# A graph layer on one core: search ahead of everything, no branch and no copies of the edges, a gather that waits for a maximum, and other moves

## The chip, the cores and the metric

The kernel runs on one core of a Trainium2 chip. The metric is the device time of one execution in microseconds (us). The core's engines run in parallel, each on its own queue of instructions: TensorE (PE, with the loading of weights shown apart as PEld), VectorE (DVE), ScalarE (ACT), GpSimd (POOL) and SyncE (SP). Transfers are issued by SP, ACT and POOL. Each queue is served in order, and an instruction that waits for a semaphore holds all that stand behind it on its engine.

## The reference, cut to what matters

```
theta_x = (x_dst - x_src) @ theta_w.T + theta_b      # x_dst = x[dst], x_src = x[src]
phi_x   = x_src @ phi_w.T + phi_b
e       = relu(theta_x + phi_x)                      # one row of 256 for each edge
out     = segment_max(e, dst, num_segments=6250)     # 0 where a node has no edge
return layernorm(x + out)
```

There are 6250 nodes with 256 features in fp32, and 100000 edges. The edges come sorted by `dst`. The row of an edge is A[dst] + B[src], with A = x·thetaᵀ plus both biases and B = x·(phi − theta)ᵀ. Since A is the same for all edges of a node, the maximum over a node's edges is A plus the maximum of the B rows of its sources.

## The kernel before, in words

**B.** At the start x is read in shares of four columns of 128 nodes (`x_q`, loads by SP), transposed on PE, copied by ACT, multiplied (L764) and stored as `b_rows` in DRAM by 13 stores that ACT issues (L784).

**Two parts.** Part 1 are the first 1130 nodes: eight columns of 128 and a rest, called `LAST`, so nine columns. Part 2 are the last 5120 nodes: 40 columns.

**Part 1** cuts its edges into 128 chunks of 146 steps, one chunk for each partition. POOL fetches one step of all chunks with one indirect DMA (L513): two groups of eight steps from x, which are then turned into B in place, and 130 steps from `b_rows`. DVE keeps a running maximum along the steps (L691), and the rows go to `maxima_1`. A node's result is the row of its last step; its place is worked out in `node_place` and `places_1`.

**Part 2** first builds a table of edges by node on DVE (`fill_table`, L930 on). For this it needs the window of 800 edges that belongs to each partition's nodes: `search_edges` (L615 to L647) finds where it begins with two small matmuls and counts, and `gather_run` fetches `dst_w` and `src_w` from there. The source nodes are cut into 17 slots of 383 rows. For two slots at a time, `choice` (L990 on) picks at most one edge per node and slot; `wanted` transposes the chosen rows on PE (L1034) and stores them as `chosen_rows`. A slot has five parts of 1024 nodes, 85 in all. `slot_part` loads the chosen rows spread over the partitions (`want`, L1061), makes one-hots from them (`hot`, by ACT in an Abs and a Relu at L1067 and L1068, or by DVE at L1065), and PE multiplies them with the slot's B rows (`terms`), 24 matmuls of 512 columns a part (L1075). DVE takes the maximum into `acc` (L1086).

**The list.** Edges that no slot took go to a list. `list_pieces` packs their words on DVE and writes them to DRAM (L1212); three `list_run` gathers read them back in even chunks. Then come 232 gathers of B rows (`list_src`), with their maxima (L691) written to `maxima_2`. The loop over the 30 list groups of eight gathers also issues the slot parts that are left, evenly over the groups.

**The end.** `rows_of` (L1270 on) loads x for up to eight columns (`x_f`, five tiles in `x_ring`), gathers a row from `maxima_1` or `maxima_2` for each column, and a `piece` of two columns makes A on PE (x transposed at L1292, two products a column at L1299, the bias at L1302), transposes `acc` (L1309) for part 2 and adds up. `normalise` (L1318 on) makes the layer norm and stores the rows. `Shares` interleaves the pieces with the norms. `LAST` is done within the last four list groups; part 1's eight columns and part 2's 40 (in widths 8, 8, 8, 4, 4, 4, 2, 2) come after the list.

**What sets the order.** A scheduler places the instructions of each engine by the order in which the program issues them and by extra dependencies written by hand: `in_turn` keeps POOL's DMAs in the order of the program; `behind_in_order` puts an instruction behind another on the same engine without a semaphore. `next_group_1` issues a group of part 1's gathers, the maxima of the group before it, a `node_place` and some slot parts. The gathered rows live in `gathered`, a ring of six tiles of eight steps.

**The start.** Besides loading the edges' `dst` in two layouts, ACT's queue copies `dst` and `src` to `dst_list` and `src_list` in DRAM and writes pads behind them. DVE counts descents in `dst`; at L653 every engine reads that count, and a branch at L654 sorts the edges if it isn't zero. With the given edges it is zero, and the branch is not taken. A second branch, at the kernel's end, takes a general path if any assumption failed.

Of the kernel before, what the change touches and what calls it, by code (L numbers as in the profile page):

```python
# [55 lines left out]
STEPS = 8  # L56
RING = 6
# [17 lines left out]
EARLY_STEPS = 6  # L75
X_RING = 5
# [351 lines left out]
def gnn_kernel(ctx: ExitStack, tc: tile.TileContext, x, src, dst, theta_w, theta_b, phi_w, phi_b, out):  # L428
# [72 lines left out]
    paced = [0]  # L501
# [14 lines left out]
    def gather(to, table, offsets):  # L516
        one = indirect(to, table, bass.IndirectOffsetOnAxis(ap=offsets, axis=0))
        for _ in range(paced[0]):
            in_turn(iota(pause, 1, 0, 0))
        return one  # L520
# [14 lines left out]

    def gather_group(i, table, a=0, b=STEPS):
        t0, n = groups[i]
        if i not in ring_tiles:
            ring_tiles[i] = gathered.tile([P, STEPS, D], FP, name="g")
        return [  # L540
            gather(ring_tiles[i][:, k, :], table, src_1[:, t0 + k : t0 + k + 1]) for k in range(a, min(b, n))
        ]

    gather_group(of_x[0], x, 0, EARLY_STEPS)


    dst_1 = const.tile([P, T1 + 2], I32, name="dst_1")
    early = body.enter_context(ExitStack())
    search = early.enter_context(tc.tile_pool(name="search", bufs=1))
# [5 lines left out]
    whole = [[E // P, P], [1, E // P]]  # L555
    rest = [[E % P, 1], [1, E % P]]
    pads = const.tile([P, 2, 8], I32, name="pads")
    nc.vector.memset(pads[:, 0, :], 0)
    nc.vector.memset(pads[:, 1, :], ID_MASK)
# [7 lines left out]
    ident = const.tile([P, P], FP, name="ident")  # L567
    make_identity(nc, ident)
    ones = const.tile([P, 1], FP, name="ones")
    nc.vector.memset(ones, 1.0)  # L570
    flags = const.tile([1, 2], I32, name="flags")
# [14 lines left out]
    first_node = const.tile([P, 1], FP, name="first_node")  # L586
    iota(first_node, 0, N1, TILES)
    columns = const.tile([P, 3, P], FP, name="columns")
    iota(columns[:, 0, :], Q1, 0, 0)
    iota(columns[:, 1, :], 1, P * Q1, 0)  # L590
    iota(columns[:, 2, :], TILES, N1 - 1 + TILES, 0)
    lowest_rows = search.tile([P, 2 * D], FP, name="lowest_rows")
    nc.vector.memset(lowest_rows, LOWEST)
    nc.sync.dma_start(maxima_1[NONE_1 : NONE_1 + 1, :], lowest_rows[0:1, :D])
    nc.sync.dma_start(maxima_2[0:1, :], lowest_rows[0:1, :D])
    list_pads = search.tile([4, OWN_LIST], I32, name="list_pads")
    nc.vector.memset(list_pads, PAD_WORD)
    nc.sync.dma_start(flat(list_words, 0, [[OWN_LIST, 1], [1, OWN_LIST]]), list_pads[:1, :])
    nc.sync.dma_start(flat(list_words, (P + 1) * OWN_LIST, [[OWN_LIST, 3], [1, OWN_LIST]]), list_pads[:3, :])
    bad = const.tile([P, 9], FP, name="bad")  # L600

    descents = search.tile([P, T + 1], FP, name="descents")
    nc.vector.tensor_tensor(descents, dst_i[:, : T + 1], dst_i[:, 1:], op=ALU.is_gt)
    n_descents = search.tile([P, 1], FP, name="n_descents")
    nc.vector.tensor_reduce(n_descents, descents, AX.X, ALU.add)
    add_up(n_descents, flags[:, 0:1])

    ids = search.tile([P, T + 2], FP, name="ids")  # L610
# [10 lines left out]

    def search_edges():

        nc.vector.tensor_copy(ids[:, : T + 1], dst_i[:, 1:])
        iota(ids[:, T + 1 :], 0, 0, T)
# [3 lines left out]
        nc.vector.tensor_scalar(hot0, columns[:, 2, :], low0, None, op0=ALU.is_ge)  # L629
        nc.vector.scalar_tensor_tensor(hot0, columns[:, 2, :], ids[:, T : T + 1], hot0, op0=ALU.is_lt, op1=ALU.mult)  # L630
        cut = 2 * D
        for i, (a, b, n) in enumerate(((cut, T + 2, T), (0, cut, cut))):
            pp = misc()
            nc.tensor.matmul(pp[:, : b - a], hot0, ids[:, a:b], start=True, stop=True)
            nc.vector.tensor_scalar(
                descents[:, a:n], pp[:, : n - a], last_node, None, op0=ALU.is_le, op1=ALU.add, accum_out=counts[:, i : i + 1]
            )
# [3 lines left out]
        nc.vector.tensor_scalar(window, counts[:, 0:1], float(E - WINDOW), None, op0=ALU.min)  # L641
# [7 lines left out]
    with (  # L649
        tc.tile_pool(name="sort", bufs=1) as sort,  # L650
        tc.tile_pool(name="ps_sort", bufs=2, space=PSUM) as ps_sort,
    ):
        n_unsorted = nc.values_load(flags[0:1, 0:1])  # L653
        with tc.If(n_unsorted > 0):  # L654
            sort_edges(nc, sort, ps_sort, src, dst, src_list, dst_list, ident)
            load_chunks(nc.sync, dst_i, dst_list, T, EDGES)
            load_chunks(nc.sync, dst_1, dst_list, T1, EDGES)
            load_rows(nc.scalar, src_1, src_list, P * T1)
            latest[0] = None
            gather_group(of_x[0], x)  # L660
            search_edges()
    latest[0] = None
# [4 lines left out]


    ids_1 = const.tile([P, T1 + 3], FP, name="ids_1")
    nc.vector.tensor_copy(ids_1[:, : T1 + 2], dst_1)  # L670
# [11 lines left out]
    def run(part, g, n, caps, t0, to, gathers=(), carry_row=None):  # L682


        for k in range(n):
            t = t0 + k if part == 1 else LIST_CHUNK - 1 - t0 - k
            if last[part] is not None:
# [10 lines left out]
                if part == 2 and latest_part[0] is not None:  # L698
                    behind_in_order(one, latest_part[0], "VectorE's order")
            last[part] = g[:, k, :]  # L700
# [14 lines left out]
    with (  # L715
        tc.tile_pool(name="prep", bufs=1) as prep,
        tc.tile_pool(name="x_in", bufs=4) as x_in,
# [8 lines left out]
        for i, b in enumerate((theta_b, phi_b)):  # L726
            nc.sync.dma_start(biases[:, i, :], flat(b, 0, [[0, P], [1, D]]))
        bias = prep.tile([P, D], FP, name="bias")
        rest = prep.tile([P, D], FP, name="rest")
        high_part = prep.tile([P, D], FR, name="high_part")  # L730
        nc.vector.tensor_add(bias, biases[:, 0, :], biases[:, 1, :])
        nc.vector.tensor_copy(high_part, bias)
        nc.vector.tensor_tensor(rest, bias, high_part.bitcast(FP), op=ALU.subtract)
        nc.vector.tensor_scalar(bias, high_part.bitcast(FP), ident[:, 0:1], None, op0=ALU.mult)
        nc.vector.scalar_tensor_tensor(bias_terms, rest, ident[:, 1:2], bias, op0=ALU.mult, op1=ALU.add)
        pick_one = prep.tile([P, 1], FP, name="pick_one")
        nc.vector.tensor_add(pick_one, ident[:, 0:1], ident[:, 1:2])
        nc.vector.tensor_copy(pick, pick_one.to_broadcast([P, P]))
        nc.vector.tensor_sub(w_in[:, 0], w_in[:, 0], w_in[:, 1])
        for i in range(2):  # L740
            for c in range(KC):
# [3 lines left out]
                nc.vector.tensor_copy(weights[:, :, i, c * P : (c + 1) * P], ps[:, 0])  # L745
# [520 lines left out]
    def gather_carry():  # L1266
# [3 lines left out]
        return carry_row  # L1270


    def rows_of(part, j0, n, ps_tile):


        share = part, j0, n
# [221 lines left out]
```

## Time and profile before

| | us |
|---|---|
| median of three runs | 727.39 |
| lowest, highest | 723.31, 733.8 |
| profiled execution | 728.03 |
| its span | 726.2 |
| busy: PE | 623.0 (86%) |
| busy: DVE | 623.9 (86%) |
| busy: ACT | 485.5 (67%) |
| busy: POOL | 486.0 (67%) |

The span is the time from the first to the last instruction that the profile shows. The profiled execution has its own time, 1.8 us over its span, and it is this execution whose rows are added up below. A row of a group reads: line, engine, operation, output and inputs with their shapes, how often, then busy time, mean nanoseconds of one, and the idle time of the engine ahead of them with what ended most of it. A row of a timeline reads: start, duration, engine, line, operation, and in square brackets how long the engine stood idle before and what released it.

### The profile page before, as it was taken

The numbers are of one execution on the slowest core, as the hardware profiler recorded it, in microseconds if no ns is written. First come the engines' busy times: TensorE is split into PE (matmuls) and PEld (weight loads), VectorE is DVE, ScalarE is ACT, GpSimd is POOL, SyncE is SP. The second block draws the span as 40 slices with busy tenths as digits, with TensorE's granted clock in tenths as the row PEclk, the third lists the DMA queues.
The fourth block names the chain that finished last, engine by engine and source line by source line (L and its number), as shares of the span: only waits on it lengthen the run. The fifth ranks groups of instructions, "written<-read, shape, count | busy, mean of one in ns | idle before, by whom it ended". The sixth has DMA issues, their size and how long they took to land.

```text
span 726.2 us, 9436 instructions
## 1 busy us (share of the span) xinstructions
PE 623.0 (86%) x2826; PEld 511.7 (70%) x2826; DVE 623.9 (86%) x1199; ACT 485.5 (67%) x676; POOL 486.0 (67%) x465
## 2 busy tenths in 40 slices
PE   0599895878987699999999999999999996699943
PEld 0388783646766587788888888888888884489942
DVE  6499999999977697986699999999999977878874
ACT  0144692899996475878777777777777771047882
POOL 6430057898877777777767577777777777757720
PEclk9799997999998799999999999999999998699976
DMA  8577335556677789986468788888888886745651
GB/s 223 147 261 242 138 106 171 183 166 203 187 224 232 252 260 366 336 279 176 146 206 280 251 284 280 269 281 281 272 286 275 257 261 225 244 139 191 225 200 71
DMA packets 56465, 164.77 MB, mean 227 GB/s; under 512 B 11899, under 2 KB 19860, under 8 KB 49332
## 3 DMA queue, kind: packets, MB, share of 16 engines
q1 hardware_dynamic: 32920, 98.76, 39.8%
q0 software_dynamic: 20944, 57.62, 27.2%
q10 hardware_dynamic: 2540, 7.69, 3.0%
q8 instruction: 25, 0.41, 0.2%
q14 instruction: 36, 0.29, 0.1%
HBM read 101.08 MB, written 63.74 MB: 227 GB/s over the span
## 4 chain that ended last, share of the span: by engine, by line
PE 55%; DVE 16%; DMA 12%; POOL 6%; issue 6%; ACT 3%; SPq 0%; DVEq 0%; POOLq 0%; ACTq 0%
PE ps_f L1075 45%; POOL g L513 6%; PE ps_e L1299 5%; DMA g<-b_rows,src 3%; DMA want<-chosen_rows 2%; DVE words L968 2%; DVE g L691 2%; DMA g<-b_rows,list_src 2%; DVE acc L1086 1%; PE ps_e L1292 1%; DVE work L965 1%; ACT hot L1067 1%; PE ps_e L1309 1%; DMA dst_w<-dst_list,window 1%; PE ps_b L764 1%
## 5 line engine op out<-in xcount | busy, mean ns | idle before, releaser
L1075 PE MATMUL ps_f<-hot,terms 128*128 128x512 f32 x1960 | 469.0, 400 | 33.2 <-DVE acc L1086 12.9
L1075 PEld LDWEIGHTS ps_f<-hot,terms 128*128 128x128 f32 x1960 | 376.4, 194 | 120.1 <-DVE acc L1086 15.1
L513 POOL DMA_INDIRECT g<-b_rows,list_src x232 | 235.8, 1016 | 73.5 <-issue 61.7
L1067 ACT ACTIVATE hot<-want,minus_row 128x1024 fp32r<-128x1024 f16 x176 | 193.9, 1149 | 95.6 <-PE ps_f L1075 80.4
L513 POOL DMA_INDIRECT g<-b_rows,src x130 | 168.0, 1292 | 92.4 <-DMA want<-chosen_rows 53.4
L1086 DVE TENSOR_TENSOR acc<-acc,ps_f 128x1024 f32<-128x1024 f32 x160 | 193.8, 1218 | 25.9 <-PE ps_f L1075 24.5
L691 DVE SCALAR_TENSOR_TENSOR g<-g,caps 128x256 f32<-128x256 f32 x376 | 181.7, 483 | 20.0 <-DMA g<-b_rows,src 12.3
L1068 ACT ACTIVATE hot<-hot 128x1024 fp32r<-128x1024 f32 x176 | 176.3, 1048 | 0.0
L513 POOL DMA_INDIRECT g<-maxima,place x49 | 47.3, 965 | 20.2 <-issue 13.7
L764 PE MATMUL ps_b<-weights,x_t 128*128 128x256 f32 x260 | 59.7, 384 | 0.7 <-ACT x_t L754 0.4
L1065 DVE TENSOR_SCALAR hot<-want,row_id 128x1024 fp32r<-128x1024 f16 x69 | 52.8, 766 | 7.2 <-DMA want<-chosen_rows 7.2
L764 PEld LDWEIGHTS ps_b<-weights,x_t 128*128 128x128 f32 x260 | 48.6, 192 | 8.4 <-ACT x_t L754 2.3
L1299 PE MATMUL ps_e<-weights,x_t 128*128 128x256 f32 x192 | 49.2, 385 | 0.2 <-ACT x_t L1294 0.2
L1299 PEld LDWEIGHTS ps_e<-weights,x_t 128*128 128x128 f32 x192 | 33.5, 194 | 3.8 <-ACT x_t L1294 0.5
L1329 ACT ACTIVATE squares<-x_f,r 128x256 bf16<-128x256 f32 x49 | 24.3, 500 | 17.0 <-DVE r L1326 17.0
L1294 ACT COPY x_t<-ps_e 128x512 f32<-128x512 f32 x24 | 13.7, 574 | 28.4 <-PE ps_e L1292 28.4
L767 ACT COPY b_sb<-ps_b 128x512 f32<-128x512 f32 (+1 forms) x25 | 14.5, 579 | 25.2 <-PE ps_b L764 25.2
L1344 ACT ACTIVATE x_f<-x_f,r 128x256 f32<-128x256 f32 x41 | 21.5, 591 | 9.9 <-DVE r L1336 9.9
L513 POOL DMA_INDIRECT g<-in_x_dram,src x16 | 19.7, 1232 | 9.5 <-issue 7.0
L1292 PE MATMUL ps_e<-ident,x_f 128*128 128x128 f32 x96 | 14.8, 280 | 11.6 <-DMA x_f<-in_x_dram 9.7
L1302 PE MATMUL ps_e<-bias_terms,pick 128*128 128x256 f32 x48 | 22.7, 473 | 0.0
L754 ACT COPY x_t<-ps_xt 128x512 f32<-128x512 f32 (+1 forms) x33 | 17.8, 593 | 6.2 <-PE ps_xt L752 6.0
(256 smaller groups left out, 435.0 us busy)
## 6 DMA issues: line engine op xcount, KB each, us to landing
maxima<-g SPq DMA_DIRECT2D x47, 1024.0 KB, 5.0
want<-chosen_rows SPq DMA_DIRECT2D x85, 256.0 KB, 4.8
x_q<-in_x_dram SPq DMA_DIRECT2D x12, 512.0 KB, 4.2
b_rows<-b_sb ACTq DMA_DIRECT2D x12, 512.0 KB, 3.5
raw<-b_rows SPq DMA_DIRECT2D x16, 256.0 KB, 4.4
x_f<-in_x_dram SPq DMA_DIRECT2D x4, 1024.0 KB, 8.9
out_dram<-x_f SPq DMA_DIRECT2D x4, 1024.0 KB, 4.4
g<-b_rows,list_src POOLq DMA_INDIRECT x232, 4.7
```

What stands on the lines that cost most here:

```text
L513: in_turn(nc.gpsimd.indirect_dma_start(out=out, out_offset=out_offset, in_=in_, in_offset=in_offset))
L691: one = nc.vector.scalar_tensor_tensor(g[:, k, :], last[part], caps[:, t : t + 1], g[:, k, :], op0=ALU.min, op1=ALU.max)
L764: nc.tensor.matmul(ps[:, h, :], x_t[:, h, k, :], weights[:, k, 0, :], start=(k == 0), stop=(k == KC - 1))
L1065: nc.vector.tensor_scalar(hot[:, b, :], want, row_id[:, b : b + 1], None, op0=ALU.is_equal)
L1067: nc.scalar.activation(hot[:, b, :], want, AF.Abs, bias=minus_row[:, b : b + 1], scale=1.0)
L1068: nc.scalar.activation(hot[:, b, :], hot[:, b, :].bitcast(FP), AF.Relu, bias=1.0, scale=-1.0)
L1075: nc.tensor.matmul(ps[:, w : w + 512], terms[:, part, b, h * P : (h + 1) * P], hot[:, b, w : w + 512], start=(i == 0), stop=(i == n - 1),)
L1086: latest_part[0] = nc.vector.tensor_tensor(to, to, ps, op=ALU.max).ins.name
L1292: nc.tensor.transpose(ps[:, 2 * i + c, :], x_f[:, k + i, c * P : (c + 1) * P], ident)
L1299: nc.tensor.matmul(a[:, i, :], x_t[:, 2 * i + c, :], weights[:, c, 1, :], start=(c == 0), stop=False)
L1302: nc.tensor.matmul(a[:, i, :], pick, bias_terms, start=False, stop=True)
L1329: nc.scalar.activation(squares, x_f[:, k, :], AF.Square, bias=mean[:, k : k + 1], scale=1.0, accum_out=var[:, k : k + 1])
```

## The change

What it does, in seven parts:

1. The search for the windows comes first. The copies to `dst_list` and `src_list`, their pads and the branch that sorts at L654 are removed; the windows are gathered straight from `dst` and `src`. The descents are counted into a tenth column of `bad`, so that the branch at the end sees them, and the sort moves into that branch. POOL makes the constants of the search ahead of its first gathers. The bias, the lowest rows and the list's pads move behind the fourth load of x.
2. On PE the transposes of x stand behind the search's product. The first slot part is issued after the fifth `choice`, the rest as before.
3. The blocks of one part that ACT makes get one Relu together; `want` has three buffers; in the last four list groups DVE makes no one-hots.
4. From group 13 of `list_pieces` on, every gather with an even number in its group waits for an earlier use: `used[k - 9]`, counted from the end of the uses issued so far. Four groups of part 1's gathers (32) move from behind the three `list_run` gathers to ahead of them.
5. Part 1's nine columns are done within the list loop, from its group 10 on; their gathered rows use tiles of `x_ring`. Shares of part 2 narrower than eight share a tile of `x_f`, so that five tiles hold all 40 columns.
6. The bias is one product for two columns, and comes first.
7. A place is kept from going below zero.

The diff's core:

```diff
+AHEAD_OF_RUNS = 4
+EARLY_SHARES = 10
+TERMS_BEHIND = 4
+X_AHEAD = 4
+WANTS = 3
...
+    used = []
+    held = [False]
+
+    def gather(to, table, offsets, k=None):
+        one = nc.gpsimd.indirect_dma_start(
+            out=to, out_offset=None, in_=table, in_offset=bass.IndirectOffsetOnAxis(ap=offsets, axis=0)
+        )
+        in_turn(one)
+        if held[0] and k is not None and k % 2 == 0:
+            after = mybir.DependencyInfo(mybir.DependencyClass.Sync, mybir.DependencyReason.DATA)
+            tc.add_manual_dep(one.ins, used[k - STEPS - 1], after, reason="rows that are used")
+        return latest[0]
...
-    for i, (to, edges) in enumerate(((dst_list, dst), (src_list, src))):
-        nc.scalar.dma_start(flat(to, 0, whole), flat(edges, 0, whole))
-        if E % P:
-            nc.scalar.dma_start(flat(to, E - E % P, rest), flat(edges, E - E % P, rest))
-        nc.scalar.dma_start(flat(to, E, [[8, P], [1, 8]]), pads[:, 1 - i, :])
...
+        one = nc.vector.tensor_tensor(descents, dst_i[:, : T + 1], dst_i[:, 1:], op=ALU.is_gt)
+        behind_in_order(one, found.ins.name, "search ahead of the edges' order")
+        nc.vector.tensor_reduce(n_descents, descents, AX.X, ALU.add)
...
-        gather_run(dst_w, dst_list, window)
-        gather_run(src_w, src_list, window)
+        gather_run(dst_w, dst, window)
+        gather_run(src_w, src, window)
...
-        n_unsorted = nc.values_load(flags[0:1, 0:1])
-        with tc.If(n_unsorted > 0):
-            sort_edges(nc, sort, ps_sort, src, dst, src_list, dst_list, ident)
...
+                weights_made = nc.vector.tensor_copy(weights[:, :, i, c * P : (c + 1) * P], ps[:, 0])
+                if i == 1:
+                    behind_in_order(weights_made, window_found[0], "search ahead of theta")
...
+                    one = nc.tensor.transpose(ps[:, h, k, :], rows[:, h, k * P : (k + 1) * P], ident)
+                    behind_in_order(one, search_product[0], "search ahead of B")
...
+        for number, share in enumerate(shares(4)):
+            if number == X_AHEAD:
+                bias_and_pads()
...
+        of_dve = min(dve_hots[0], blocks)
         for b in range(blocks):
...
                 nc.scalar.activation(hot[:, b, :], want, AF.Abs, bias=minus_row[:, b : b + 1], scale=1.0)
-                nc.scalar.activation(hot[:, b, :], hot[:, b, :].bitcast(FP), AF.Relu, bias=1.0, scale=-1.0)
+        if of_dve < blocks:
+            apart = hot[:, of_dve:blocks, :]
+            nc.scalar.activation(apart, apart.bitcast(FP), AF.Relu, bias=1.0, scale=-1.0)
...
+        at = j0 % STEPS if part == 2 else 0
+        if at == 0:
+            x_tiles[part] = x_ring.tile([P, STEPS, D], FP, name="x_f")
+        x_f = x_tiles[part][:, at : at + n, :]
...
+        m = x_ring.tile([P, STEPS, D], FP, name="x_f") if part == 1 else gathered.tile([P, STEPS, D], FP, name="g")
...
+            nc.tensor.matmul(a[:, :w, :], pick, bias_of.to_broadcast([P, w, D]), start=True, stop=False)
...
-                nc.tensor.matmul(a[:, i, :], pick, bias_terms, start=False, stop=True)
...
+        if s0 == TERMS_BEHIND * BATCH_S:
+            fetch_parts(1)
...
+        elif i == 13:
+            held[0] = True
+            for _ in range(AHEAD_OF_RUNS):
+                next_group_1(1)
...
+    def first_shares():
+        for share in (LAST, (1, 0, Q1)):
+            pieces, norm = rows_of(*share, misc)
+            for piece in pieces:
+                for _ in piece:
+                    yield
+            yield from norm
...
-            early_share = Shares(misc)
-            early_share.add(*LAST)
-            early_share.finish()
+            dve_hots[0] = 0
+        if i >= EARLY_SHARES:
+            next(early_shares, None)
...
-    for share in [(1, 0, Q1)] + last_shares:
+    for share in last_shares:
         at_end.add(*share)
...
+            sort_edges(nc, sort, ps_sort, src, dst, src_list, dst_list, ident)
         general_path(tc, x, theta_w, pick, bias_terms, out, b_rows, src_list, dst_list, ident, E)
```

More of the change, by code (lines that the diff above doesn't have):

```diff
@@ L540, in gather_group @@
         return [
-            gather(ring_tiles[i][:, k, :], table, src_1[:, t0 + k : t0 + k + 1]) for k in range(a, min(b, n))
+            gather(ring_tiles[i][:, k, :], table, src_1[:, t0 + k : t0 + k + 1], k) for k in range(a, min(b, n))
         ]
-    gather_group(of_x[0], x, 0, EARLY_STEPS)
-    dst_1 = const.tile([P, T1 + 2], I32, name="dst_1")
+    first_node = const.tile([P, 1], FP, name="first_node")
+    columns = const.tile([P, 2, P], FP, name="columns")
     early = body.enter_context(ExitStack())
     search = early.enter_context(tc.tile_pool(name="search", bufs=1))
+    ids = search.tile([P, T + 2], FP, name="ids")
+    starts = search.tile([P, P], FP, name="starts")
+    ident = const.tile([P, P], FP, name="ident")
+    in_turn(nc.gpsimd.memset(ident, 0.0))
+    in_turn(
+        nc.gpsimd.affine_select(
+            out=ident,
+            in_=ident,
+            compare_op=ALU.not_equal,
+            fill=1.0,
+            base=0,
+            pattern=[[-1, P]],
+            channel_multiplier=1,
+        )
+    )
+    in_turn(iota(starts, TILES, N1 - 1 + TILES, 0))
+    in_turn(iota(first_node, 0, N1, TILES))
+    in_turn(iota(ids[:, T + 1 :], 0, 0, T))
+    gather_group(of_x[0], x, 0, EARLY_STEPS)
+    dst_1 = search.tile([P, T1 + 2], I32, name="dst_1")
     dst_i = search.tile([P, T + 2], I32, name="dst_i")
@@ L640, in search_edges @@
         nc.vector.tensor_scalar(counts[:, 0:1], end, -float(WINDOW), 0.0, op0=ALU.add, op1=ALU.max)
[L641 removed]
+        one = nc.vector.tensor_scalar(window, counts[:, 0:1], float(E - WINDOW), None, op0=ALU.min)
         nc.vector.tensor_scalar(bad[:, 0:1], end, float(WINDOW), None, op0=ALU.is_lt)
[L643 to L644 removed]
+        window_found[0] = one.ins.name
+        gather_run(dst_w, dst, window)
+        gather_run(src_w, src, window)
+        windows_fetched[0] = latest[0]
     search_edges()
     gather_group(of_x[0], x, EARLY_STEPS)
[L649 to L652, printed above, removed]
[L653 to L662 removed]
+    ids_1 = const.tile([P, T1 + 3], FP, name="ids_1")
+    one = nc.vector.tensor_copy(ids_1[:, : T1 + 2], dst_1)
+    behind_in_order(one, window_found[0], "search ahead of the first part")
     early.close()
@@ L699, in run @@
                     behind_in_order(one, latest_part[0], "VectorE's order")
+                used.append(one.ins.name)
             last[part] = g[:, k, :]
@@ L910, in gnn_kernel @@
     )
-    iota(order, 1, 1, 0)
+    behind_in_order(iota(order, 1, 1, 0), windows_fetched[0], "runs ahead of the ranks")
     padded, unused = table("padded", I16), table("unused", I16)
@@ L1263, in gather_2 @@
         columns_of = [LIST_CHUNK - 1 - t0 - k for k in range(n)]
-        return g, [gather(g[:, k, :], b_rows, list_src[:, t : t + 1]) for k, t in enumerate(columns_of)]
+        return g, [gather(g[:, k, :], b_rows, list_src[:, t : t + 1], k) for k, t in enumerate(columns_of)]
     def gather_carry():
@@ L1299, in piece @@
                     nc.tensor.matmul(
[L1300 removed]
+                        a[:, i, :], x_t[:, 2 * i + c, :], weights[:, c, 1, :], start=False, stop=(i == w - 1 and c == KC - 1)
                     )
[L1302 removed]
             some = m[:, k : k + w, :]
```

120 lines of the change are left out of this document (53 added, 67 removed).

## The prediction

> **What bounds the kernel now.** I read the page's chain by engines first (the top row below), then the windows of all engines by stage, then the gathers alone.
>
> ```profile
> PE 55%; DVE 16%; DMA 12%; POOL 6%; issue 6%; ACT 3%; SPq 0%; DVEq 0%; POOLq 0%; ACTq 0%
> ...
> 0.00:29.70 29.70, 4.66 (x12) 2.40 (x12) 13.21 (x44) 1.28 (x1) 16.00 (x32) 0.91 0.69 193
> 29.70:97.50 67.80, 63.19 (x337) 54.90 (x338) 65.66 (x112) 35.79 (x65) 11.03 (x11) 0.97 0.58 198
> 97.50:214.90 117.40, 92.82 (x389) 70.58 (x388) 113.02 (x219) 101.03 (x147) 98.94 (x63) 0.94 0.57 177
> 214.90:310.10 95.20, 82.04 (x325) 65.53 (x324) 75.92 (x152) 61.91 (x67) 73.72 (x75) 0.89 0.87 291
> 310.10:440.00 129.90, 129.90 (x575) 107.24 (x574) 109.82 (x155) 100.97 (x102) 94.60 (x94) 1.00 0.74 234
> 440.00:600.00 160.00, 160.00 (x707) 132.24 (x706) 150.82 (x233) 123.28 (x123) 123.33 (x121) 1.00 0.85 271
> 600.00:639.40 39.40, 25.32 (x92) 19.26 (x92) 32.93 (x60) 4.14 (x8) 29.73 (x30) 0.78 0.68 223
> 639.40:726.20 86.80, 65.12 (x399) 59.58 (x397) 62.52 (x230) 57.13 (x167) 38.60 (x40) 0.89 0.50 168
> ```
>
> The columns are the window, its length, then busy time (and instructions) of PE, weight loads, DVE, ACT and POOL, the granted clock, the DMA share and GB/s. Four limits follow each other: until 29.7 the search for the window of edges, until 214.9 DVE (65.66 of 67.80, then 113.02 of 117.40), in the list stages PE at 100% with DVE close behind, and an end of 86.8 us. Modelled matmul ends make PE look fuller than it is, so POOL has to be looked at by itself:
>
> ```profile
> 214.91 0.71 SPq L1212 DMA_DIRECT2D list_words<-work  x1
> ...
> 97.50:214.90 117.40, 97.97 (x62) 0.94 0.57 177
> 214.90:310.10 95.20, 72.86 (x72) 0.89 0.87 291
> 440.00:600.00 160.00, 123.33 (x121) 1.00 0.85 271
> 627.48 1.12 POOL L513 DMA_INDIRECT g<-b_rows,list_src  x1 [0.30 <-issue]
> 628.91 0.94 POOL L513 DMA_INDIRECT g<-maxima,place  x1 [0.30 <-issue]
> ```
>
> The windows here are of L513 on POOL alone. Gathers leave it back to back: 0.95 us and 0.30 us of issue make 1.25. They take 117.40/62 = 1.89 us each up to 214.9, 95.20/72 = 1.32 next, 160/121 = 1.32 in the list. POOL is never told "100%", yet nearly every gather waits for issue alone. I take POOL's order as the pace, with PE and DVE within a few per cent of it.
>
> ```profile
> L513 POOL DMA_INDIRECT g<-b_rows,list_src x232: 942/948/1489, 310.1 to 627.5; - x116
> L513 POOL DMA_INDIRECT g<-b_rows,src x130: 942/972/7739, 97.5 to 308.9; - x130
> L513 POOL DMA_INDIRECT g<-maxima,place x49: 940/946/1161, 606.7 to 693.9; - x49
> 639.39 0.42 DVE L689 TENSOR_TENSOR g<-g,heads 128x256 f32<-128x256 f32 x1
> ```
>
> So the first b_rows gather (97.5), the last list gather (627.5), the last maximum (639.4) and the end (726.2) are the posts on which the sum hangs.
>
> **1. Start: search first, no branch, no copies.**
>
> ```profile
> 1.65 5.47 DMA w_in<-in_L_gnn_theta_w_dram
> 8.05 6.51 DMA dst_list<-pads
> ...
> 22.32 0.95 POOL L513 DMA_INDIRECT dst_w<-dst_list,window  x1 [6.89 <-DVE window L641]
> 25.76 1.51 PE L744 MATMUL ps_xt<-ident,w_in 128*128 128x128 f32 x6 [5.08 <-DVEq L654]
> 29.72 0.64 DVE L939 TENSOR_SCALAR wide<-dst_w,first_node 128x800 f32<-128x800 int32 x1 [3.58 <-DMA dst_w<-dst_list,window]
> L784 ACTq DMA_DIRECT2D b_rows<-b_sb x13: 325/327/476, 35.5 to 93.3; - x13
> ```
>
> The top two rows are of the chain in order of time. Before, PE's first transposes of the weights wait for the branch (L654) at 25.8, the first store of B leaves at 35.5, the last at 93.3, and the first b_rows gather stands 4.2 us behind it. After, no branch holds PE; the weights land at 1.65 + 5.47 = 7.1. The window loses the copies' landing (6.51) and comes at 22.3 − 6.5 = 16; by the order of the instructions theta's copies stand behind it on DVE, and PE starts x at about 17 less what it can do ahead of them. From PE's release to the first store were 9.7 us; PE's work on the weights, about half of that, is now done while DVE searches, so I put the first store at 18, 17 us sooner. PE no longer breaks off B for the `chosen` transposes (L1034) nor ACT for hots, so of the 93.3 − 35.5 = 57.8 us I let 5 go as well: last store at 71, first b_rows gather at 75, or 23 us sooner. The bounds are the window's 6.5, if B waits for all that the search issues, and 25.8 − 7.1 + 5 = 24. The bias operations (L737 to L742) now stand in DVE's queue ahead of the table and wait for a load that SP issues behind four x loads; the table, whose edges land 7.4 us after the window is asked for, starts at 22 to 24 instead of 29.7. The lowest rows and list pads move behind x on SP's queue; their readers come hundreds of us later and the price is nothing.
>
> **2. Hots.** One Relu over two or three blocks replaces two or three; the row of the old form is 1048 ns.
>
> ```profile
> L1067 ACT ACTIVATE hot<-want,minus_row 128x1024 fp32r<-128x1024 f16 x176 | 193.9, 1149 | 95.6 <-PE ps_f L1075 80.4
> L1068 ACT ACTIVATE hot<-hot 128x1024 fp32r<-128x1024 f32 x176 | 176.3, 1048 | 0.0
> L1065 DVE TENSOR_SCALAR hot<-want,row_id 128x1024 fp32r<-128x1024 f16 x69 | 52.8, 766 | 7.2 <-DMA want<-chosen_rows 7.2
> ```
>
> ACT waits 95.6 us ahead of hots, 80.4 of them for PE, so its time is covered in both directions: 0, and at most the 7.2 us that DVE waited for `want` with the third buffer. In the last four list groups DVE gives its hot (0.77 us a part) back to ACT: some 8 parts, 6 us of DVE gained, 8 × (1.15 + 1.05) = 18 us of ACT, both beside PE. I take 0. The first slot part behind the fifth `choice` moves PE and ACT work, and one terms subtraction on DVE, within a stretch that DVE limits, and the clamp of the places takes a copy's place: 0 for both, at most the 6.5 us that DVE stands idle from 29.7 to 214.9.
>
> **3. Ahead of the list.** POOL has 104 instead of 72 b_rows gathers ahead of the three runs that fetch the list, and 26 instead of 58 behind. With 1.89 us each from 75 on, (206 − 75)/1.89 = about 70 have left by 206, instead of 62 by 214.9, where the list's words left. (DVE is full up to there and starts some 7 us sooner; 4 maxima and 5 `acc` more stand ahead of the words, 8 us, for which it had 2.1 + 4.4 idle: I take 206 to 209.) What still has to leave is 130 − 70 = 60, then 3 runs, 3 for heads and carry, 232 of the list and the 9 of the first part's columns, which now stand amid the list: 307. At 1.31 us (between 1.32 and the bare 1.25, nearer to the first, which has DVE beside it) that is 402 us: the last at 608, where before the last of the list left at 627.5 and eight of the columns behind it. The runs leave when 34 more gathers have (206 + 34 × 1.31 = 250); the list's first gather stands 26 gathers and the words' handling behind, at some 288 instead of 310.
>
> **4. The hold.** From group 13 on, every even gather waits for the maximum about 17 columns back, and POOL's whole queue waits with it, the heads, the carry and the first part's columns too. At 1.31 us apart, 17 columns are 22 us of cover. Before, a lead of up to 48 (six tiles of eight) was possible, and once it was used:
>
> ```profile
> 310.00:360.00 50.00, 4.16 (x9) 1.00 0.67 202
> 360.00:440.00 80.00, 31.23 (x65) 1.00 0.78 254
> L691 DVE SCALAR_TENSOR_TENSOR g<-g,caps 128x256 f32<-128x256 f32 x376 | 181.7, 483 | 20.0 <-DMA g<-b_rows,src 12.3
> ```
>
> The windows are of the maxima (L691) on DVE: 9 in 50 us, while POOL, at 1.32, issued about 38 gathers. In the changed order DVE has 18 maxima between its 51st and 61st `acc` where it had 4, so the lull is mostly filled. The hold's price is between 0 and (38 − 17 − 14) × 1.31 = 9 us, since 14 more maxima free 14 more gathers. Below 0: fewer gathers in flight could land sooner, but DVE stood 20.0 us ahead of its maxima in all, the most that can come back. I take 2, already in the 1.31.
>
> That the whole queue waits has a rule beside it: the Trainium skill, DMA: Bandwidth & Descriptors, Anatomy of one DMA — SWDGE (gpsimd) path, says that any semaphore wait happens on the issuing sequencer before dispatch, and that DMA engines do not wait. By it a held gather holds every later one, never only itself, which speaks against this edit; no row of before shows a hold of this kind, and the third rival below is what it would make.
>
> **5. The heavy stretch.** Between 97.5 and 214.9 single gathers take several times their usual length beside DVE's work on the list:
>
> ```profile
> 155.70 7.74 POOL L513 DMA_INDIRECT g<-b_rows,src  x1 [0.30 <-issue]
> 163.74 5.25 POOL L513 DMA_INDIRECT g<-b_rows,src  x1 [0.30 <-DVE g L691]
> 164.73 1.87 DVE L1203 COPY_PREDICATED work<-words,work 128x1432 int32<-128x1432 int32 x1
> ```
>
> That is why I use 1.89 and not 1.32 for every gather before 206. The Trainium skill, SBUF — State Buffer, SBUF: two separate sides, says that a GpSimd DMA's descriptors cannot be written while a two-port DVE instruction holds the shared port. The rows agree as far as they go (7.74 and 5.25 us against 0.95); by it the early gathers of the new 75 to 97 would meet the choice's instructions in the same way, which is half of the first rival below.
>
> **6. End.**
>
> ```profile
> 639.40:644.40 5.00, 5.00 (x32) 4.58 (x31) 2.60 (x8) 1.17 (x2) 0.00 (x0) 1.00 0.67 262
> 644.40:695.00 50.60, 50.60 (x322) 46.80 (x321) 41.91 (x144) 39.80 (x119) 38.60 (x40) 1.00 0.60 191
> 644.41 0.94 POOL L513 DMA_INDIRECT g<-maxima,place  x1 [5.61 <-DMA maxima<-g]
> 707.46 1.09 PE L1292 MATMUL ps_e<-ident,x_f 128*128 128x128 f32 x4 [9.74 <-DMA x_f<-in_x_dram]
> L1302 PE MATMUL ps_e<-bias_terms,pick 128*128 128x256 f32 x48 | 22.7, 473 | 0.0
> ```
>
> From the last maximum the last rows take 5.0 us to be written, the 40 gathers 50.6 (1.27 each), and the rest 31.2, in which PE stands 9.74 for an x tile whose place an output still held. Shared x tiles cover all 40 columns, so that wait goes. Late next are the last gathered rows and one pair's chain: from that transposition to the end are 726.2 − 707.5 = 18.7, of which I let about 3 (x transposed and copied) lie ahead: 16. Eight columns of part 1 (four pairs of 14 matmuls, 32 of which take PE 5.0 us: 9 in all) leave the end for the list, where PE is full. One wide bias product per pair saves between 0 and 0.47 us of PE, 20 pairs; I take 0.2 (4 us), hidden behind POOL's 50.6, which is the longer of the two once part 1 has gone. After: 5 + 50.6 + 16 = 72, or 15 less. Those 9 us of PE in the list can be a loss of as much, if PE is the pace; the 25.32 of 39.40 at 600 to 639.4 say that it has 14 us of room, and I take 0.
>
> **Sum.** Last list-stage gather at 608, its landing and the last group's maxima 10 more (before, 639.4 − 627.5 = 12): 618. With 72 the span is 690, against 726.2. The profiled execution took 728.03, 1.8 around the span: 691.8, and I say 691, as that run stands 0.1% over the median of 727.39. About 2%, or 14.5 us, is what a measurement here tells from no change.
>
> **Rivals.**
> - **The early start is lost.** Gathers from 75 on run in the stretch where DVE is full and take 2.2 us or more each, or PE and DVE, full until 600, pace the list themselves and get part 1's columns on top. For it: 129.90 of 129.90 and 150.82 of 160. Against it: PE and DVE start 7 us or more sooner too. Then the last maximum stays at 639.4 and only the end pays: 639.4 + 72 + 1.8 = 713. That would also be the change not doing what it says at its start. Chance 0.18.
> - **Gathers at the bare pace.** With fewer in flight and DVE eased each takes 1.26: 307 × 1.26 = 387, last at 593, last maximum at 602; with 2 us off the end, 602 + 70 + 1.8 = 674. Against it: DVE's 150.82 of 160. Chance 0.12.
> - **The hold turns into a stop (slower).** If the lull stays as it was (9 maxima in 50 us), POOL stands for it all, 38 × 1.31 = 50 us, and the list comes late by as much: 691 + 50 = 741. It decides once DVE makes no maximum for more than the 22 us of cover; it turns the sign at 36 us of such loss. For it: the queue is in order, and DVE's maxima wait in turn for `acc` and so for PE. Against it: 18 maxima for 4. Chance 0.07.
>
> **How the numbers follow.** My forecast, 678 to 704, has 0.63. The range of 666 to 716 takes in nearly all of the first two rivals' times and leaves out the hold and the ends, about 0.18. Faster by over 2% is below 713: the forecast, the second rival and half of the first, 0.84; within 2% the other half and a light hold, 0.11; slower by over 2%, 0.05.
>
> **What will show it.** Right: the first b_rows gather near 75, the first list gather near 288, the last maximum near 618, no wait for x_f behind 640, and 72 us from the last maximum to the end. Wrong: gathers of over 2 us before 206, POOL waiting for maxima (L691) by more than some 10 us, or PE waiting in the list for hots from ACT. The forecast falls if the last maximum stays at 639, or if the stretch behind it still takes 80.

## The result and the profile after

The changed kernel takes 702.43 us (median of four, 697.79 to 702.92); the ratio to the kernel before is 0.9645, with a 95% interval of 0.9558 to 0.9733. The prediction said 691, with a range of 666 to 716. The profiled execution took 702.37, its span is 700.2. Eight of the twelve runs below were made on two chips on which every kernel, the one before too (914 to 959 us), takes some 20 to 30% longer; they are read only against each other, and single times given for those two chips are medians that leave out runs more than 1.5% above the fastest of their kernel.

The windows of all engines by stage, of the changed kernel, cut at its own posts (columns as in the prediction):

```profile
0.00:24.00 24.00, 15.39 (x57) 11.57 (x58) 18.44 (x60) 5.40 (x9) 18.38 (x33) 1.00 0.88 268
24.00:79.20 55.20, 54.91 (x296) 47.67 (x296) 53.40 (x81) 28.55 (x53) 12.11 (x11) 1.00 0.62 216
79.20:213.00 133.80, 108.64 (x445) 84.65 (x443) 127.05 (x241) 116.12 (x133) 100.54 (x77) 0.91 0.58 185
213.00:289.50 76.50, 67.91 (x283) 53.97 (x281) 67.24 (x144) 58.50 (x49) 59.23 (x62) 0.96 0.84 266
289.50:440.00 150.50, 150.50 (x668) 124.30 (x667) 133.82 (x208) 117.84 (x94) 112.62 (x112) 1.00 0.82 262
440.00:600.00 160.00, 154.37 (x684) 125.95 (x682) 136.17 (x229) 122.48 (x115) 122.63 (x123) 1.00 0.86 283
600.00:624.30 24.30, 16.85 (x63) 12.46 (x64) 21.04 (x29) 8.37 (x10) 9.76 (x11) 0.79 0.46 161
624.30:700.20 75.90, 56.12 (x314) 49.17 (x312) 53.64 (x200) 46.32 (x138) 38.23 (x40) 0.87 0.46 156
```

PE starts within the first stage now (15.39 us busy before 24, where it had 4.66 before 29.7). The groups of gathers, which name the first and the last of each kind, give the posts (the helper that records them is L523 now, and the stores of B are L796):

```profile
L796 ACTq DMA_DIRECT2D b_rows<-b_sb x13: 241/327/363, 18.2 to 73.1; - x13
...
L523 POOL DMA_INDIRECT g<-b_rows,list_src x232: 942/946/1901, 289.5 to 611.9; - x116
L523 POOL DMA_INDIRECT g<-b_rows,src x130: 942/948/3902, 79.2 to 287.8; - x130
L523 POOL DMA_INDIRECT g<-maxima,place x40: 942/946/1183, 628.8 to 678.0; - x40
```

From the timeline, the list's words leaving, the longest hold of a gather, the end of the list's maxima and the wait of POOL for them to be written:

```profile
206.82 0.94 POOL L523 DMA_INDIRECT g<-b_rows,src  x1 [10.74 <-DVE g L684]
213.18 0.34 SPq L1227 DMA_DIRECT2D list_words<-work  x1
609.29 10.47 DVE L1101 TENSOR_TENSOR acc<-acc,ps_f 128x1024 f32<-128x1024 f32 x9
619.68 4.12 DVE L684 SCALAR_TENSOR_TENSOR g<-g,caps 128x256 f32<-128x256 f32 x8
623.84 0.42 DVE L682 TENSOR_TENSOR g<-g,heads 128x256 f32<-128x256 f32 x1
628.80 0.94 POOL L523 DMA_INDIRECT g<-maxima,place  x1 [15.99 <-DMA maxima<-g]
```

| post, us | before | predicted | after |
|---|---|---|---|
| first b_rows gather | 97.5 | 75 | 79.2 |
| list's words leave | 214.9 | 206 to 209 | 213.2 |
| first list gather | 310.1 | 288 | 289.5 |
| last list gather | 627.5 | 608 | 611.9 |
| last maximum | 639.4 | 618 | 623.8 |
| from there to the end | 86.8 | 72 | 76.4 |

The first gather is 18.3 us sooner and the list's first 20.6, but not through the words, which are only 1.7 us sooner. What the early start bought is 76 gathers ahead of them instead of 62: fourteen at 1.32 us are 18.5. That holds although the hold's wait of 10.74 us (0.30 of it the usual issue) lies in the same stretch. By the last list gather 15.6 are left.

### The profile page after: what moved, and what is told of

The parts are those of the page before. It is cut to its first block, busy times and chain, and to the rows that moved or that the text cites. A ratio compares the mean times of both kernels' runs of the same rounds, so it can differ in the third digit from the quotient of the medians.

```text
span 700.2 us, 9338 instructions
## 1 busy us (share of the span) xinstructions
PE 624.7 (89%) x2800; PEld 509.8 (73%) x2800; DVE 610.8 (87%) x1185; ACT 503.6 (72%) x596; POOL 473.5 (68%) x465
## 5 line engine op out<-in xcount | busy, mean ns | idle before, releaser
L523 POOL DMA_INDIRECT g<-b_rows,list_src x232 | 232.7, 1003 | 74.9 <-issue 45.9
L1080 ACT ACTIVATE hot<-want,minus_row 128x1024 fp32r<-128x1024 f16 x187 | 205.6, 1147 | 96.4 <-PE ps_f L1090 90.2
L523 POOL DMA_INDIRECT g<-b_rows,src x130 | 155.0, 1192 | 90.8 <-DMA want<-chosen_rows 41.6
L1083 ACT ACTIVATE hot<-hot 128x2048 fp32r<-128x2048 f32 (+2 forms) x85 | 177.6, 2089 | 1.8
L523 POOL DMA_INDIRECT g<-maxima,place x40 | 38.2, 956 | 27.9 <-DMA maxima<-g 16.0
L1078 DVE TENSOR_SCALAR hot<-want,row_id 128x1024 fp32r<-128x1024 f16 x58 | 44.2, 762 | 0.0
L1320 PE MATMUL ps_e<-weights,x_t 128*128 128x256 f32 x160 | 39.7, 393 | 0.4 <-ACT x_t L1313 0.4
L523 POOL DMA_INDIRECT g<-in_x_dram,src x16 | 23.2, 1447 | 5.6 <-issue 4.4
L1330 DVE TENSOR_TENSOR g<-g,ps_e 128x512 f32<-128x512 f32 x20 | 13.7, 686 | 12.8 <-DMA g<-maxima,place 10.4
```

What stands on the lines that cost most here:

```text
L523: one = nc.gpsimd.indirect_dma_start(out=to, out_offset=None, in_=table, in_offset=bass.IndirectOffsetOnAxis(ap=offsets, axis=0))
L1078: nc.vector.tensor_scalar(hot[:, b, :], want, row_id[:, b : b + 1], None, op0=ALU.is_equal)
L1080: nc.scalar.activation(hot[:, b, :], want, AF.Abs, bias=minus_row[:, b : b + 1], scale=1.0)
L1083: nc.scalar.activation(apart, apart.bitcast(FP), AF.Relu, bias=1.0, scale=-1.0)
L1320: nc.tensor.matmul(a[:, i, :], x_t[:, 2 * i + c, :], weights[:, c, 1, :], start=False, stop=(i == w - 1 and c == KC - 1))
```

## The experiments

### The hold

Taking it away leaves nearly the whole order of every engine as it is.

```diff
         elif i == 13:
-            held[0] = True
             for _ in range(AHEAD_OF_RUNS):
```

On the first of the two longer chips, and on the second:

> The changed kernel without the hold: no gather waits for a use, the rest and nearly the whole order of every engine as it is. Theory 1 (POOL's queue paces the list, so its waits for maxima are paid for): the changed kernel's POOL stands 26.1 us for maxima, of which one wait of 10.7 us lies just ahead of the list's words; without them the three runs leave some 10 us sooner and the end comes 8 to 14 us sooner: 688 to 695. Rival (DVE and PE pace, the hold only makes POOL wait where its rows would lie unused): 700 to 705, and the waits turn up elsewhere on POOL. Second rival (the hold earns something, since without it more rows are in flight than are used and other transfers land later): 706 or more.

> No gather waits for a use. Theory 1 (POOL's queue paces the list): 8 to 14 us less than the changed kernel beside it. Rival (DVE and PE pace): within 3 us of it. Second rival (the hold earns something): more than 3 us slower; the run before gave 882 where three kernels with a hold gave 832 to 837 on the same chip, which was slow for all, and by that this rival is ahead.

Beside them, a hold that starts with the list loop only, and the changed kernel itself:

```diff
         elif i == 13:
-            held[0] = True
...
     early_shares = first_shares()
+    held[0] = True
```

> The hold begins with the list loop and not with group 13 of the list's pieces, so only the early wait of 10.7 us goes and the list's own waits for maxima (13.2 us, of which all but some 5 is the usual issue) stay. Theory 1: within 5 us of the run without any hold, 690 to 698. Rival (it is the list's hold that matters): 700 to 705, as the changed kernel.

> The changed kernel itself, unedited, beside the kernel before and the next three on one chip: the measure for them. Its ratio to the kernel before was 0.9645 (0.9558 to 0.9733); theory: the same ratio, 0.956 to 0.973, whatever the chip. Rival (the gain depends on how late transfers and instructions come on a chip): a ratio outside of that.

On the first of these chips the kernel without the hold took 880.7 us and the one with the late hold 833.1; on the second the kernel without it took 890 (887 and 894) and the changed kernel 837.1. There the hold earns some 48 to 53 us, the second rival. The late hold was not beside the full hold on one chip, but it lies as far below the kernel without any, so it seems to be the list's part of it that counts. The kernel before took 916.6 to 959.4 in its seven runs on the second chip, so the changed kernel's ratio there lies between 837.1/959.4 = 0.873 and 837.1/916.6 = 0.913, outside of 0.956 to 0.973: the rival of that run. That could not be carried over to a chip on which the kernel before takes 726, so the pair was run once more on a third:

> The changed kernel unedited, as the measure for the two beside it, on whatever chip this is. Theory (chips differ in how long PE is stopped once PE, DVE, ACT and the gathers are all at work): on a chip where the kernel before takes some 726 us this takes 697 to 705; where it takes some 940 us, 827 to 840. Rival (the two chips of the other runs were odd ones out in another way): any other pair of times.

> No gather waits for a use. On a chip where the kernel before takes some 726 us: theory 1 (POOL's queue paces the list) 8 to 14 us less than the changed kernel beside it; the second rival (the hold earns something) more than 3 us above it. Where it takes some 940 us: 45 to 65 us above it, as in the two calls before.

Here the kernel before took 723.85 us, the changed one 701.13 (ratio 0.9662, 0.9589 to 0.9736), and without the hold 689.87 (0.9500, 0.9431 to 0.9569): 11.3 us less, theory 1 (the two profiled executions are 8.6 apart). The waits of the whole run, three of POOL's waits beyond the usual 0.30 us, and the groups of gathers, first with the hold (the changed kernel on this chip):

```profile
POOL g L523 <- DVE g L684: 19.4, 38, 3.7
DVE g L684 <- DMA g<-b_rows,list_src: 18.6, 13, 6.4
DVE g L684 <- DMA g<-b_rows,src: 5.5, 2, 3.8
...
202.96 0.94 POOL L523 DMA_INDIRECT g<-b_rows,src  x1 [3.70 <-DVE g L684]
312.32 1.21 POOL L523 DMA_INDIRECT g<-b_rows,list_src  x1 [1.70 <-DVE g L684]
324.26 0.94 POOL L523 DMA_INDIRECT g<-b_rows,list_src  x1 [1.83 <-DVE g L684]
...
L523 POOL DMA_INDIRECT g<-b_rows,list_src x232: 940/947/1900, 285.3 to 608.5; - x116
619.76 0.42 DVE L682 TENSOR_TENSOR g<-g,heads 128x256 f32<-128x256 f32 x1
```

and without it:

```profile
POOL g L523 <- DVE g L684: 4.0, 13, 0.3
DVE g L684 <- DMA g<-b_rows,list_src: 12.5, 11, 3.3
...
L523 POOL DMA_INDIRECT g<-b_rows,list_src x232: 942/947/1906, 279.5 to 599.8; - x116
610.79 0.42 DVE L682 TENSOR_TENSOR g<-g,heads 128x256 f32<-128x256 f32 x1
```

A row of waits names who waited for whom, the sum in us, how often, and the longest. With the hold POOL's row for maxima is 15.4 us longer, but most of its 38 waits are the usual 0.30 us of issue, which the row puts down to a maximum that ended last. What exceeds 0.30 us is six waits: 3.4 us in one ahead of the list and 4.4 in five within it, 7.8 in all; without the hold there is none (the longest is 0.3). DVE in turn waits 11.6 us more for rows (24.1 against 12.5): each stands for the other. The last list gather comes 8.7 us later and the last maximum 9.0, though the list's words leave 4.9 us sooner with the hold (209.3 against 214.2): without it 85 gathers have left by then, with it 76. Of the late hold, which keeps the five small waits only, there is no run on a chip like this one.

### Part 1's columns after the list

```diff
-        for share in (LAST, (1, 0, Q1)):
+        for share in (LAST,):
             pieces, norm = rows_of(*share, misc)
...
-        m = x_ring.tile([P, STEPS, D], FP, name="x_f") if part == 1 else gathered.tile([P, STEPS, D], FP, name="g")
+        m = x_ring.tile([P, STEPS, D], FP, name="x_f") if share == LAST else gathered.tile([P, STEPS, D], FP, name="g")
...
-    for share in last_shares:
+    for share in [(1, 0, Q1)] + last_shares:
```

> The eight columns of part 1 are done after the list again, only LAST within it. Theory 1 (they were on PE's path at the end, 9 to 11 us of it, and the list, paced by POOL, gains less by losing them): 5 to 11 us slower than the changed kernel; eight gathers leave the list (10 us of POOL) and come back ahead of the end's 40, so the last maximum should come up to 10 us sooner and the stretch behind it be longer by 14 to 20. Rival (moved work is worth the same in either place): within 3 us.

> The eight columns of part 1 after the list. On a chip where the kernel before takes some 726 us: theory 1 (POOL paces the list, PE the end) the last maximum up to 10 us sooner, the stretch behind it 14 to 20 us longer, 5 to 11 us slower in all. Where it takes some 940 us, PE is what the list waits for, and the run before gave 6 us less: 2 to 10 us less than the changed kernel.

On the second longer chip it took 831.0 us beside 837.1, on the third chip 696.46 (0.9565, 0.9491 to 0.9639) beside 701.13: less on both, by 6 and 4.7 us, where theory 1 said 5 to 11 more. That is a small difference on each chip, but of one sign, and theory 1 is off. The row of the first of the 48 gathers behind the list, on the third chip, and the end of its list:

```profile
L523 POOL DMA_INDIRECT g<-b_rows,list_src x232: 940/947/1902, 290.7 to 601.8; - x116
610.27 1.07 POOL L523 DMA_INDIRECT g<-maxima,place  x1 [7.49 <-DVE g L684]
613.70 0.42 DVE L682 TENSOR_TENSOR g<-g,heads 128x256 f32<-128x256 f32 x1
```

The list takes 601.8 − 290.7 = 311.1 us instead of 323.2: eight gathers of POOL's and part 1's pieces less. The end grows by 4.5 only (694.4 − 613.7 = 80.7, against 696.0 − 619.8 = 76.2), not by 14 to 20, since the eight gathers lie where POOL otherwise waits 15 to 16 us for the last maxima to be written; and PE does part 1's pairs in the same time. Even so they are late here: the hold keeps the first of them 7.5 us.

### The branch

The branch alone, at its old place; the copies of the edges stay away.

```diff
         nc.vector.tensor_reduce(n_descents, descents, AX.X, ALU.add)
+        add_up(n_descents, flags[:, 1:2])
...
+        n_unsorted = nc.values_load(flags[0:1, 1:2])
+        with tc.If(n_unsorted > 0):
+            sort_edges(nc, sort, ps_sort, src, dst, src_list, dst_list, ident)
+    latest[0] = None
```

> The branch alone is put back at its old place, reading the count of descents; the copies of the edges stay away. Theory 1 (the early start of B reaches the end through POOL's queue): PE is released later, the first b_rows gather comes 4 to 10 us later than 79.2, and the time goes up by about as much: 706 to 712. Rival (the early start is lost in the stretch where DVE is full): first b_rows gather later by the same, the time 700 to 704.

> The branch alone at its old place. Theory 1: first b_rows gather 8 to 12 us later than in the changed kernel (90.1 was seen), and 4 to 12 us more in time. Rival (the early start is lost further on): within 3 us of the changed kernel.

It took 831.9 us on the first longer chip, beside 833.1 (late hold), and on the second 843 (837 to 849) beside 837.1. On the first gather it is plain, by these rows of its runs on the first and the second chip, and of the changed kernel's on the second:

```profile
L523 POOL DMA_INDIRECT g<-b_rows,src x130: 945/952/4559, 90.1 to 305.6; - x130
L523 POOL DMA_INDIRECT g<-b_rows,src x130: 942/950/3795, 91.5 to 314.6; - x130
```
```profile
L523 POOL DMA_INDIRECT g<-b_rows,src x130: 945/951/3801, 79.0 to 296.1; - x130
```

On the second chip the branch is worth 12.5 us of the first gather, where the change gained 18; on the first chip it is 8 to 12, as the kernels without it have their first gather at 78.4 to 82.2 there. The times don't tell whether that reaches the end: one pair says 6 more, the other 1 less, each within what the runs on these chips scatter. It was not tried on a chip where the kernel before takes 726; that stays open. The copies were not tried alone.

### An x tile for each share

```diff
-        if at == 0:
+        if True:
+            at = 0
             x_tiles[part] = x_ring.tile([P, STEPS, D], FP, name="x_f")
```

> Each share of the last columns takes an x tile of its own again, as before, so that later ones wait for an output to be stored; the rest stays as changed. Theory 1 (the wait for x stood on the path): the stretch from the last maximum to the end grows by 8 to 10 us: 710 to 713. Rival (PE and ACT are behind by then and hide it): 702 to 705.

835.8 us, beside 833.1 for the late hold on the same chip: no loss that shows. From the last maximum to the end it has 100.3 us where the late hold has 91.2, the 8 to 10 more of theory 1, but its last maximum comes 6.8 us sooner. PE again stands ahead of four transposes of x at the end, for a norm by this row, which the late hold's run lacks:

```profile
814.59 1.09 PE L1312 MATMUL ps_e<-ident,x_f 128*128 128x128 f32 x4 [9.66 <-DVE r L427]
```

On a chip on which the end is slowed by other waits the time settles nothing; what the profile of the changed kernel shows is that the wait for x_f is gone from it.

### Both edits that gained

> Both edits on the changed kernel: no gather waits for a use, and the eight columns of part 1 come after the list. On a chip where the kernel before takes some 726 us: theory (POOL's queue paces the list; the eight gathers then fill its wait for the last maxima to be written instead of list time, and without the hold they need not wait themselves, 7.5 us in the run with columns at the end alone) at least the sum of the two single gains, 11.3 + 4.7: 676 to 686 us, a ratio of 0.93 to 0.948 to the kernel before. Rival (both edits buy the same wait): 688 to 692. Where the kernel before takes some 940 us: 870 to 890, as the lack of the hold decides there.

681.74 us beside 725.77 for the kernel before on a fourth chip: 0.9346, 0.9254 to 0.9439. That is below the changed kernel's 0.9645 and 0.9662, with no overlap of the intervals, and within what the theory said. It is below the columns alone (0.9491 to 0.9639) as well; with the missing hold alone (0.9431 to 0.9569) the intervals still touch. Its gathers and the end of its list:

```profile
L523 POOL DMA_INDIRECT g<-b_rows,list_src x232: 942/948/1902, 281.5 to 591.0; - x116
590.99 0.94 POOL L523 DMA_INDIRECT g<-b_rows,list_src  x1 [0.30 <-issue]
592.24 0.94 POOL L523 DMA_INDIRECT g<-maxima,place  x1 [0.30 <-issue]
...
601.10 0.94 POOL L523 DMA_INDIRECT g<-maxima,place  x1 [0.30 <-issue]
607.90 1.19 POOL L523 DMA_INDIRECT g<-maxima,place  x1 [5.86 <-DMA maxima<-g]
```

Part 1's eight gathers now follow the list's last without a gap and fill POOL's wait: 5.86 us are left of the 15.99. The kernel before had them there too: by its rows in the prediction they leave from 628.91 on, and 5.61 us are left.

The merged Relu, the third `want` buffer, the first slot part behind the fifth `choice`, the four groups ahead of the runs and the wide bias product were not tried alone.

## Why the prediction was right or wrong

The direction, the range and the first terms held; the time is 11 us above the forecast, and that comes from three posts: 3.9 us at the last list gather, 2 from there to the last maximum, 4.4 behind it.

That POOL's path came out as summed is luck in part. From the first b_rows gather to the last of the list were 608 − 75 = 533 us forecast and 611.9 − 79.2 = 532.7 measured. But 14.9 of these are waits of the hold beyond the usual issue (10.4 ahead of the words, 4.4 in the list), priced at 2, and the heavy stretch gave as much back.

- **Start: right, a little large.** The first store of B leaves at 18.2 (18 said), the last at 73.1 (71), and the first gather stands 6.1 us behind it instead of 4.2.
- **The heavy stretch: no worse.** 133.8/76 = 1.76 us a gather from 79.2 to 213 against 1.89 before, and 1.62 without the hold's 10.4 us, with a longest gather of 3.9 us against 7.7. So 1.89 was too dear. One sign of being wrong, gathers of over 2 us before 206, was there (six; the kernel before has eleven up to its words), but the mean of all is what counts. The rule of the Trainium skill, SBUF — State Buffer, SBUF: two separate sides, would have let the early gathers meet the choice's instructions; gathers of 2 to 4 us are still there, so the trace doesn't speak against the rule, but the first rival's 2.2 us and more did not come.
- **Ahead of the list: right in the mechanism.** From 213.2 to 611.9 are 301 instructions on POOL, 1.325 us each, and 1.31 without the hold's 4.4 us (1.31 said). POOL's order paces the list: with the hold's waits gone from that queue, and nearly nothing else changed, the last list gather and the last maximum moved by 8.7 and 9.0 us. In three profiled executions the way from the first b_rows gather to the last of the list took 532.6, 528.0 and 518.9 us with 14.9, 7.8 and 0 us of such waits: 518 to 520 without them.
- **The hold: mis-sized, and the term that failed first.** "I take 2, already in the 1.31" was the step; alone it measures 11.3 us. I had bounded it by one lull behind 310, in the list. The first profile shows five waits there, of 0.5 to 1.8 us, and the longest, 10.74 us, ahead of the list's words, in the stretch where I priced no hold; DVE then stands longer for rows. The sign listed for this ("POOL waiting for maxima by more than some 10 us") was there. The Trainium skill's rule in DMA: Bandwidth & Descriptors, Anatomy of one DMA — SWDGE (gpsimd) path, that a semaphore wait is on the issuing sequencer ahead of the dispatch, is what the trace shows: POOL issues nothing in those 10.74 us.
- **Part 1's columns: a gain that was a loss.** The step was "Eight columns of part 1 ... leave the end for the list ... and I take 0". The 9 us of PE that leave the end were beside POOL's wait for the last maxima anyway, and I counted their eight gathers into the list's 307 as if the end would pay them back. The rows that I had shown had the answer: before, these gathers fill that wait down to 5.61 us, after, it is 15.99. Measured alone: 4.7 us the other way.
- **End: 4.4 us short.** The wait for x is gone, as said, and the 40 gathers take 49.2 us. But behind the last of them (678.0) come 22.2 us and not 16: PE and ACT are still two pairs behind when its rows land (PE's last product ends at 685.2), and the norms follow.
- **DVE's last nine `acc`** (10.47 us ahead of the last eight maxima) are late next after POOL, which the sum had only as "10 more" behind the last gather; 12 were needed.
- **Rivals.** The early start was not lost, the bare pace of 1.26 did not come, and the hold did not turn the sign; its kind was right and its size was a quarter of the rival's 50. PE's waits for hots from ACT did not grow in the list (1.1 us from 289 to 624, in the kernel before 1.2).

## What to carry to other kernels

Where one queue issues all gathers and paces a stage, a wait put on that queue is paid: here the last gather moved by nearly all of it. Bound it by every wait it can make, from the first held instruction on, and not by one lull. Before work is moved out of the last stage, look for the wait in that stage that hides it: a transfer's landing that nothing else can use was the cheapest place for it here. Measure such an edit on more than one chip before it is kept or dropped: this hold cost 11 us on one and earned some 50 on two others.

## What the runs showed of the hardware that was not expected

Of five sets of runs, two fell on chips where the kernel before takes some 940 us and not 726. Up to 212 us the changed kernel is the same there to a few tenths (first gather at 79.0 against 79.2, words leaving at 212.8 against 213.2); behind it PE stands for many us with nothing that it waits for, by the waits' rows. On the chips where it takes 726 there is no such row for PE's matmuls. PE's timeline of the kernel without the hold on the second of these chips, and the windows of all engines of the one with the late hold on the first:

```profile
217.25 5.28 PE L1090 MATMUL ps_f<-hot,terms 128*128 128x512 f32 x22
223.77 0.39 PE L1090 MATMUL ps_f<-hot,terms 128*128 128x512 f32 x1 [1.24 <-issue]
224.50 0.40 PE L1090 MATMUL ps_f<-hot,terms 128*128 128x512 f32 x1 [0.34 <-issue]
243.95 2.50 PE L1090 MATMUL ps_f<-hot,terms 128*128 128x512 f32 x5 [19.05 <-issue]
```
```profile
215.00:220.00 5.00, 3.30 (x15) 2.25 (x13) 2.60 (x5) 0.00 (x0) 3.78 (x5) 1.00 0.55 161
220.00:225.00 5.00, 2.34 (x5) 0.77 (x4) 0.00 (x0) 0.00 (x0) 3.78 (x5) 0.74 0.37 105
225.00:230.00 5.00, 0.00 (x0) 0.00 (x0) 0.00 (x0) 0.00 (x0) 3.78 (x5) 0.50 0.37 105
```

While PE stands, the DMA share is 0.37, so full DMA engines aren't the reason; POOL alone goes on. The granted clock of 0.50 does not tell cause from effect; it is 1.00 where PE's work first thins out, and falls while PE stands. That a hold on the gathers is worth some 48 to 53 us on these chips, and costs 11 on another, is shown. It goes with less of that standing: in the profiled executions PE's matmuls stand so for 44 us with the late hold and 82 without on the first of these chips, for 33 with the hold and 87 without on the second (the 87 in an execution of 906.4 us). Why PE stands, and why less with the hold, is open.

Holding gathers back did not make rows land sooner: the median from issue to landing of POOL's gathers is 4.8 us with the hold and 4.9 without it on the third chip.
